# A Haar-domain channel mix as two half-height products, and column transforms as one full-precision product

## The chip, the core and the metric

The kernel runs on one core of one Trainium2 chip. The metric is the device time of one execution in microseconds (us). The engines are called PE (TensorE, the matrix engine; PEld is its weight load), DVE (VectorE), ACT (ScalarE), POOL (GpSimd) and SP (SyncE). SP and ACT issue the DMAs here.

## The reference

The input x has 4 images of 64 channels and 256 x 256 pixels. Four layers are applied in a row. Layers 0, 1 and 3 are long convolutions: for each channel a separable filter, a product of a row filter and a column filter that come out of a small sine network, is convolved with the image (causally: the FFT of twice the size makes it a plain convolution cut to 256 x 256), and the input times a bias per channel is added. Layer 2 works in the Haar domain:

```python
f1 = haar2d(x)
acc = 0
for i in range(2):
    f3 = f1 * v[i]
    f4 = einsum('bchw,oc->bohw', f3, conv_w[i])
    f5 = sign(f4) * relu(abs(f4) - tau[i])
    acc = acc + f5
y = haar2d(acc, inverse=True) + x
```

v and tau have one value per pixel of the coefficient image, and conv_w[i] is a 64 x 64 matrix over the channels. So at every coefficient the 64 channels are mixed by two matrices, thresholded, and the two results are added.

## The kernel before, in words

**Convolutions.** For one image b and one channel c, `contract` (L187) multiplies the 256 x 256 image with a Toeplitz matrix read from a padded filter in DRAM. It issues, for each of two halves of the output rows, one product with 256 columns (L190) and one with 128 (L191), both in full 32-bit precision, which PE executes as two instructions each. Layer 0 and layer 1 take two contractions each. `first` copies the result out of PSUM on ACT (L199), `second` adds bias times input on DVE (L212).

**Forward Haar transform.** `pairs` (L253) makes the first row level on DVE (L257, L258), `store` keeps a copy in DRAM, `levels` (L263) makes the other row levels on DVE. The column transform `down` (L283) is one product with a 128 x 128 matrix of signs. A channel in the set `in_parts` is first split: `split` (L276) rounds the 128 x 512 tile to fp32r on ACT (L280) and takes the rest on DVE (L281), and `down` then runs two fp32r products with `hbr` on the two exact parts (L288). A channel outside the set takes one full-precision product with `hbt` instead. Before the change every channel of every image is in `in_parts`. The result is copied by ACT (L296) and stored to DRAM (coef).

**Mixing.** `mixing` (L316) takes a group of four coefficient rows at a time, 64 groups per image. `load` brings a tile f with (row half k, channel c) on the 128 partitions, two such rows q, 256 columns. `mix` (L335) multiplies, for q and for each half h of the columns, the 128 x 128 block of f (as weights) with `wb`, a 128 x 256 block-diagonal matrix that holds the 64 x 128 pair of channel matrices twice and zeros elsewhere (L340). The result px fills two banks of PSUM. DVE (L357) and ACT (L359) multiply it with v, 64 elements at a time on ACT: 12 of 16 blocks for images 0 to 2, 6 for image 3. `shrink` takes the absolute value and the sign on ACT (L365, L366) and subtracts tau on DVE (L367), `signed` finishes the threshold on DVE (L372), `add` adds the two results into the SBUF array z on DVE (L376).

**Inverse.** `inverse` (L386) gathers one channel at a time out of z on ACT (zc, L396), transforms rows (L403, L404) and columns (L416), adds the kept input and runs layer 3 on two thirds of the channels; for images 0 to 2 the other third (`put_off`) is stored and its layer 3 is run during the mixing of image 3.

**Order.** All work is put on a list of events with a tick, a place within the tick, and a function; the list is sorted and issued, so that the order on each engine is fixed by ticks written out by hand. The mixing of image b has one group per tick. Beside it run the convolutions of image b + 1, spread over the ticks from shortly before the mixing to its end; channels of the last two blocks of four are stretched out into the inverse (`border`). In image 3 the layer 3 convolutions put off earlier run beside the mixing.

Of the kernel before, what the change touches and what calls it, by code (L numbers as in the profile page):

```python
# [9 lines left out]
F32 = mybir.dt.float32  # L10
# [6 lines left out]
B, C, S, EMB, ORD = 4, 64, 256, 33, 64  # L17
P = 128
# [19 lines left out]
def conv_seq_kernel(ctx, tc, x, fz, fw, bias, decay, haar, haar_row, factors, vt, taut, wmix, out):  # L38
# [14 lines left out]
    nc = tc.nc  # L53

    const = ctx.enter_context(tc.tile_pool(name="const", bufs=1))
# [3 lines left out]
    zpool = ctx.enter_context(tc.tile_pool(name="zpool", bufs=1))  # L59
# [4 lines left out]
    psx = ctx.enter_context(tc.tile_pool(name="psx", bufs=2, space=PSUM))  # L64
# [4 lines left out]
    hbr = const.tile([P, P], F32R, name="hbr")  # L69
    hrow = const.tile([P, 2, P], F32, name="hrow")  # L70
    hsinv, ident = hrow[:, 0, :], hrow[:, 1, :]
    wb = const.tile([P, 2, P], F32, name="wb")
    bsb = const.tile([P, 3, C], F32, name="bsb")


    z = zpool.tile([P, 2, S, C], F32, name="z")

    sd = zpool.tile([P, 8, 2, 2, P], F32, name="sd")
    keep = [dram.tile([C, P, 2, 2, P], F32, name=f"keep{b}") for b in range(B)]
# [4 lines left out]

    room = z.rearrange("p h r c -> p (h r c)")
    free = [0]

    def part(n, parts=P):  # L90
# [57 lines left out]
    def constants():  # L148
        signs = part(P)
        nc.sync.dma_start(hbt, haar[0])  # L150
        nc.sync.dma_start(signs, haar[1])
        nc.sync.dma_start(hrow, haar_row)
        nc.vector.memset(wb, 0.0)
        for r in range(2):
            nc.sync.dma_start(wb[r * C : (r + 1) * C, r, :], wmix)
        nc.scalar.copy(hb, signs)
        nc.scalar.copy(hbr, hbt)

# [57 lines left out]

    def butterfly(b):

        d = mx.tile([P, 2, C], F32, name=f"bfly_{b}", tag="mag")
        nc.vector.tensor_sub(d, z[:, :, 0, :], z[:, :, 1, :])  # L220
        nc.vector.tensor_add(z[:, :, 0, :], z[:, :, 0, :], z[:, :, 1, :])
        nc.vector.tensor_copy(z[:, :, 1, :], d)

# [90 lines left out]
    def mixing(b, start, n_act):  # L316

        st = {}

        def load(g):  # L320
            f = mx.tile([P, 2, S], F32, name=f"f_{b}_{g}", tag="f", bufs=3)
            nc.sync.dma_start(f, coef[b].rearrange("k c p w -> (k c) p w")[:, 2 * g : 2 * g + 2])
            st[g] = {"f": f}
            if g % GT == 0:
                t = mx.tile([P, 2, GT, 16], F32, name=f"vt_{b}_{g}", tag="vt")
                nc.sync.dma_start(t, scales[g // GT])
                st["vt", g // GT] = t

        def scale(g, i):
            return st["vt", g // GT][:, i, g % GT, :]  # L330

        def over(g, i, n):
            return scale(g, i)[:, :n].unsqueeze(2).to_broadcast([P, n, C])

        def mix(g):  # L335
            f = st[g]["f"]
            ps = psx.tile([P, 2, 2, S], F32, name=f"px_{b}_{g}", tag="mix")
            for q in range(2):
                for h in range(2):
                    nc.tensor.matmul(  # L340
                        ps[:, h, q, :],
                        f[:, q, h * P : (h + 1) * P],
                        wb.rearrange("p r n -> p (r n)"),
                        start=True,
                        stop=True,
                    )
            if g == 0:

                one, two = ps[:, :, 0, :P], ps[:, :, 0, P:]
                d = mx.tile([P, 2, P], F32, name=f"d_{b}", tag="mag")  # L350
                nc.vector.tensor_copy(d, two)
                nc.vector.tensor_sub(two, one, d)
                nc.vector.tensor_add(one, one, d)
            f4 = mx.tile([P, 16, C], F32, name=f"f4_{b}_{g}", tag="f4")
            px = ps.rearrange("p h q (r i o) -> p (h q r i) o", r=2, i=2)
            n = 16 - n_act
            nc.vector.tensor_tensor(f4[:, :n], px[:, :n], over(g, 0, n), ALU.mult)  # L357
            for j in range(n, 16):
                nc.scalar.mul(f4[:, j], px[:, j], scale(g, 0)[:, j : j + 1])  # L359
            st[g]["f4"] = f4  # L360

        def shrink(g):
            f4 = st[g]["f4"]
            mag = mx.tile([P, 16, C], F32, name=f"mag_{b}_{g}", tag="mag")
            nc.scalar.activation(mag, f4, AF.Abs)  # L365
            nc.scalar.activation(f4, f4, AF.Sign)  # L366
            nc.vector.tensor_sub(mag, mag, over(g, 1, 16))  # L367
            st[g]["mag"] = mag

        def signed(g):  # L370
            mag = st[g]["mag"]
            nc.vector.scalar_tensor_tensor(mag, mag, 0.0, st[g]["f4"], ALU.max, ALU.mult)  # L372

        def add(g):
            parts = st.pop(g)["mag"].rearrange("p (h r i) o -> p h r i o", h=2, i=2)
            nc.vector.tensor_add(z[:, :, 4 * g : 4 * g + 4, :], parts[:, :, :, 0, :], parts[:, :, :, 1, :])  # L376

        for g in range(S // 4):
            at(start + g - 2, 0, load, g)

            for s, (place, stage) in enumerate([(-2.5, mix), (-3.5, shrink), (-4.1, signed), (-4.2, add)]):
                at(start + g + s, place, stage, g)

    def inverse(b, start, put_off):  # L386

        st = {}

        def fetch(c):  # L390
            if c == 0:
                butterfly(b)
            r = mx.tile([P, 2, 2, P], F32, name=f"r_{b}_{c}", tag="f", bufs=3)
            nc.sync.dma_start(r, keep[b][c])
            a = mx.tile([P, 2, 2, P], F32, name=f"zc_{b}_{c}", tag="mag")
            nc.scalar.copy(a, z[:, :, :, c].rearrange("p h (i k) -> p h k i", k=2))  # L396
            st[c] = {"r": r, "z": a}

        def rows(c):
            a = st[c]["z"]  # L400
            ps = psm.tile([P, 2, 2, P], F32, name=f"pw_{b}_{c}", tag="mm")
            for m in range(2):
                nc.tensor.matmul(ps[:, m, 0, :], a[:, 0, m, :], hsinv, start=True, stop=True)  # L403
                nc.tensor.transpose(ps[:, m, 1, :], a[:, 1, m, :], ident)  # L404
            w = mx.tile([P, 2, 2, 2, P], F32R, name=f"w_{b}_{c}", tag="f4")
            nc.scalar.copy(w[:, 0], ps)  # L406
            nc.vector.tensor_tensor(w[:, 1], ps, w[:, 0].bitcast(F32), ALU.subtract)
            st[c]["w"] = w
            if c not in put_off:
                st[c][2] = toeplitz(2, c, f"t2_{b}_{c}")  # L410

        def cols(c):
            ps = psm.tile([P, 2, 2, P], F32, name=f"pu_{b}_{c}", tag="mm")
            flat = "p m e w -> p (m e w)"
            for i in range(2):
                nc.tensor.matmul(  # L416
                    ps.rearrange(flat), hb, st[c]["w"][:, i].rearrange(flat), start=(i == 0), stop=(i == 1)
                )
            t = io.tile([P, 2, 2, P], F32, name=f"t_{b}_{c}", tag="res", bufs=BUFS["res"])
            nc.vector.scalar_tensor_tensor(t, st[c]["r"], 0.5, ps, ALU.mult, ALU.add)  # L420
            u = io.tile([P, 2, S], F32, name=f"u_{b}_{c}", tag="y", bufs=BUFS["y"])
            v = u.rearrange("p m (w e) -> p m w e", e=2)
            nc.vector.tensor_add(v[:, :, :, 0], t[:, :, 0, :], t[:, :, 1, :])
            nc.vector.tensor_sub(v[:, :, :, 1], t[:, :, 0, :], t[:, :, 1, :])
            st[c]["u"] = u

        ends = last(b, st)
        for c in range(C):

            at(start + c, -1, fetch, c)  # L430
            at(start + c + 1, -9, rows, c)
            at(start + c + 2, -8, cols, c)
            if c in put_off:
                at(start + c + 3, -5, lambda c: nc.scalar.dma_start(late[b, c], st.pop(c)["u"]), c)
            else:
                for s, stage in enumerate(ends):
                    at(start + c + 3 + s, s - 7, stage, c)
# [22 lines left out]
    def spread(begin, end, n=C):  # L460
        return [begin + i * (end - begin - 1) // (n - 1) for i in range(n)]
# [4 lines left out]
    one, two, three = filters(0, nc.scalar), filters(1, nc.scalar), filters(2, nc.sync)  # L466
# [20 lines left out]
    for b in range(B):  # L487
        mixing(b, start, 12 if b + 1 < B else 6)
        end = start + groups + 3
        if b + 1 < B:  # L490
            ready = convolutions(b + 1, spread(ahead, end + 2), in_parts=range(C), border=end)
        else:
            convolution(
                [(i, c) for i in range(B - 1) for c in sorted(put_off)], spread(start - 2, end + 2, (B - 1) * len(put_off))
            )
        inverse(b, end, put_off if b + 1 < B else ())

        start = max(end + C, ready + 3)
        ahead = start - 3
# [111 lines left out]
```

## Time and profile before

| | us |
|---|---|
| median of 3 runs | 2974.68 (2972.39 to 2974.85) |
| profiled execution, its own time | 2975.2 |
| profiled execution, span | 2973.4 |
| PE busy | 2913.8 (98%) |
| PE weight loads busy | 2615.1 (88%) |
| DVE busy | 2545.5 (86%) |
| ACT busy | 2156.9 (73%) |

The span runs from the first to the last instruction of the profiled execution; its own time also holds what lies around the span. TensorE's granted clock is full throughout. The mixing of image 0 lies from about 453 to 860 us, of image 1 from 1092 to 1526, of image 2 from 1766 to 2206, of image 3 from 2436 to 2708; the inverse stages lie between and after them.

In a line of a group the columns are: source line, engine, operation, output and inputs by name, weights' and moving shapes, count, then busy us, mean ns of one, and after the second bar the idle time of the engine just before, with what ended it. In a timeline line they are start, length, engine, line, operation, names, shapes and how many were merged.

### The profile page before, as it was taken

Reading aid. Unit: us, or ns where it says so; the run is one execution under the profiler, and the core shown is the slowest. Engines: PE = TensorE matmul, PEld = TensorE weight load, DVE = VectorE, ACT = ScalarE, POOL = GpSimd, SP = SyncE. Lnnn points to the kernel's source line nnn. Section 1 sums busy time; section 2 is a strip of 40 time slices with the busy share of each in tenths; the row PEclk is TensorE's granted clock in tenths of the full one; section 3 lists DMA queues with packets and bytes.
Section 4 is the critical chain, followed back from the end, with each engine's and each line's share of the span. In section 5 each row is a group of like instructions: output and inputs, shape, how many; then the busy total and the mean of one; then the engine's idle time right before and its main releaser. Section 6 shows DMA issues by size and latency. Waiting matters only on the chain. (4 is left out here: it accounts for less than half of the span.)

```text
span 2973.4 us, 52066 instructions
## 1 busy us (share of the span) xinstructions
PE 2913.8 (98%) x16950; PEld 2615.1 (88%) x16950; DVE 2545.5 (86%) x4571; ACT 2156.9 (73%) x5014; POOL 0.2 (0%) x4
## 2 busy tenths in 40 slices
PE   8999999999999999999999999999999999999999
PEld 6898988888888898888888988888888988888998
DVE  5766768999998879999989879999998889998776
ACT  2333338999986758889986668989986768887554
POOL 0000000000000000000000000000000000000000
PEclk9999999999999999999999999999999999999999
DMA  5877777666667876776777876777777878777676
GB/s 159 247 237 226 229 228 212 203 202 207 207 196 244 250 217 200 208 216 204 208 219 244 250 225 197 209 210 211 207 216 237 256 236 235 233 230 217 212 212 186
DMA packets 562497, 649.73 MB, mean 219 GB/s; under 512 B 44369, under 2 KB 447412, under 8 KB 562100
## 3 DMA queue, kind: packets, MB, share of 16 engines
q1 hardware_dynamic: 482996, 562.07, 64.8%
q10 hardware_dynamic: 79232, 84.34, 8.0%
q8 instruction: 137, 2.24, 0.3%
q14 instruction: 132, 1.08, 0.1%
HBM read 426.77 MB, written 219.48 MB: 217 GB/s over the span
## 5 line engine op out<-in xcount | busy, mean ns | idle before, releaser
L190 PE MATMUL py<-t,a 128*128 128x256 f32 x3072 | 919.0, 381 | 8.9 <-ACT a L199 5.5
L199 ACT COPY a<-pa 128x512 f32<-128x512 f32 x768 | 477.2, 621 | 387.9 <-PE pa L191 357.2
L359 ACT ACTIVATE f<-px,vt 128x64 f32<-128x64 f32 x2688 | 582.3, 358 | 143.5 <-DVE f L357 143.4
L191 PEld LDWEIGHTS py<-t,a 128*128 128x128 f32 x3072 | 583.4, 190 | 79.3
L191 PE MATMUL py<-t,a 128*128 128x128 f32 x3072 | 590.0, 274 | 0.0
L190 PEld LDWEIGHTS py<-t,a 128*128 128x128 f32 x3072 | 500.4, 191 | 50.9 <-ACT a L199 12.4
L340 PE MATMUL px<-wb,f 128*128 128x256 f32 x2048 | 488.2, 380 | 4.9 <-ACT f L359 4.9
L340 PEld LDWEIGHTS px<-wb,f 128*128 128x128 f32 x2048 | 369.5, 190 | 47.0 <-ACT f L359 6.7
L367 DVE TENSOR_TENSOR mag<-mag,vt 128x1024 f32<-128x1024 f32 x256 | 312.4, 1220 | 28.3 <-ACT mag L365 26.9
L190 PE MATMUL pa<-t,y 128*128 128x256 f32 x1024 | 311.6, 386 | 22.4 <-DVE y L212 20.3
L406 ACT CAST w<-pw 128x512 fp32r<-128x512 f32 x256 | 150.2, 587 | 227.0 <-PE pw L404 218.9
L372 DVE SCALAR_TENSOR_TENSOR mag<-mag,f 128x1024 f32<-128x1024 f32 x256 | 311.7, 1218 | 1.9
L190 PE MATMUL pa<-t,x 128*128 128x256 f32 x1024 | 305.9, 380 | 0.4 <-issue 0.4
L365 ACT ACTIVATE mag<-f 128x1024 f32<-128x1024 f32 x256 | 293.7, 1147 | 11.0 <-DVE z L376 8.8
L366 ACT ACTIVATE f<-f 128x1024 f32<-128x1024 f32 x256 | 285.2, 1114 | 3.0
L396 ACT COPY zc<-z 128x512 f32<-128x512 f32 x256 | 282.0, 1103 | 0.7 <-ACT w L406 0.4
L281 DVE TENSOR_TENSOR sp<-sd,sp 128x512 fp32r<-128x512 f32 x256 | 176.1, 688 | 91.4 <-ACT sp L280 90.2
L190 PE MATMUL pa<-t,u 128*128 128x256 f32 x772 | 232.8, 383 | 2.9 <-PE pu L416 1.6
L420 DVE SCALAR_TENSOR_TENSOR t<-r,pu 128x512 f32<-128x512 f32 x256 | 174.9, 683 | 60.4 <-PE pu L416 57.0
L212 DVE SCALAR_TENSOR_TENSOR y<-x,bsb,py 128x512 f32<-128x512 f32 x256 | 190.1, 742 | 37.9 <-PE py L191 36.1
L212 DVE SCALAR_TENSOR_TENSOR y<-y,bsb,py 128x512 f32<-128x512 f32 x256 | 190.0, 742 | 34.2 <-PE py L191 33.1
L191 PEld LDWEIGHTS pa<-t,x 128*128 128x128 f32 x1024 | 194.6, 190 | 26.3
(67 smaller groups left out, 4458.9 us busy)
## 6 DMA issues: line engine op xcount, KB each, us to landing
t<-pad SPq DMA_DIRECT2D x768, 256.0 KB, 3.9
x<-in_x SPq DMA_DIRECT2D x256, 256.0 KB, 3.6
keep<-sd SPq DMA_DIRECT2D x256, 256.0 KB, 2.9
coef<-co SPq DMA_DIRECT2D x256, 256.0 KB, 3.3
f<-coef SPq DMA_DIRECT2D x256, 256.0 KB, 3.2
r<-keep SPq DMA_DIRECT2D x256, 256.0 KB, 3.3
out_y<-y ACTq DMA_DIRECT2D x256, 256.0 KB, 3.6
late<-u ACTq DMA_DIRECT2D x63, 256.0 KB, 2.9
```

The source lines that it names most:

```text
L190: nc.tensor.matmul(ps[:, m, :], src[:, 0, m * P : (m + 1) * P], t[:, ::-1], start=True, stop=False)
L191: nc.tensor.matmul(ps[:, m, P:], src[:, 1, m * P : (m + 1) * P], t[:, : P - 1 : -1], start=False, stop=True)
L199: nc.scalar.copy(a, ps)
L212: nc.vector.scalar_tensor_tensor(y, s[res], bsb[:, layer, c : c + 1], ps, ALU.mult, ALU.add)
L281: nc.vector.tensor_tensor(w[:, 1], t, w[:, 0].bitcast(F32), ALU.subtract)
L340: nc.tensor.matmul(ps[:, h, q, :], f[:, q, h * P : (h + 1) * P], wb.rearrange("p r n -> p (r n)"), start=True, stop=True,)
L359: nc.scalar.mul(f4[:, j], px[:, j], scale(g, 0)[:, j : j + 1])
L365: nc.scalar.activation(mag, f4, AF.Abs)
L366: nc.scalar.activation(f4, f4, AF.Sign)
L367: nc.vector.tensor_sub(mag, mag, over(g, 1, 16))
L372: nc.vector.scalar_tensor_tensor(mag, mag, 0.0, st[g]["f4"], ALU.max, ALU.mult)
L396: nc.scalar.copy(a, z[:, :, :, c].rearrange("p h (i k) -> p h k i", k=2))
```

## The change

The channel mix no longer multiplies 128 rows with a block-diagonal matrix. `wb` holds the 64 x 128 pair of channel matrices twice, once on partitions 0 to 63 and once on 64 to 127, with no zeros. Each block of f is multiplied in two products of 64 rows and 128 columns, one for each half r of the partitions. The result has r as its outermost index, so that the two halves lie in different banks of PSUM. z, the scales and the factors follow with a new order of indices (r, h, q, i); sizes stay.

The set `in_parts` gets smaller beside the mixing. For image 0 it still holds all channels. For image 1 it holds channels 56 to 63. For images 2 and 3 it holds channels 56 to 63 and the even channels below 56. The other channels take the existing path with one full-precision product, and their `split` isn't issued.

```diff
-    wb = const.tile([P, 2, P], F32, name="wb")
+    wb = const.tile([P, P], F32, name="wb")
-    z = zpool.tile([P, 2, S, C], F32, name="z")
+    z = zpool.tile([P, 2, 2, P, C], F32, name="z")
...
-        nc.vector.memset(wb, 0.0)
         for r in range(2):
-            nc.sync.dma_start(wb[r * C : (r + 1) * C, r, :], wmix)
+            nc.sync.dma_start(wb[r * C : (r + 1) * C], wmix)
...
         def mix(g):
             f = st[g]["f"]
-            ps = psx.tile([P, 2, 2, S], F32, name=f"px_{b}_{g}", tag="mix")
-            for q in range(2):
-                for h in range(2):
-                    nc.tensor.matmul(
-                        ps[:, h, q, :],
-                        f[:, q, h * P : (h + 1) * P],
-                        wb.rearrange("p r n -> p (r n)"),
-                        start=True,
-                        stop=True,
-                    )
+            ps = psx.tile([P, 2, 2, 2, P], F32, name=f"px_{b}_{g}", tag="mix")
+            for h in range(2):
+                for q in range(2):
+                    for r in range(2):
+                        rows = slice(r * C, (r + 1) * C)
+                        nc.tensor.matmul(
+                            ps[:, r, h, q, :], f[rows, q, h * P : (h + 1) * P], wb[rows], start=True, stop=True
+                        )
...
-            px = ps.rearrange("p h q (r i o) -> p (h q r i) o", r=2, i=2)
+            px = ps.rearrange("p r h q (i o) -> p (r h q i) o", i=2)
...
         def add(g):
-            parts = st.pop(g)["mag"].rearrange("p (h r i) o -> p h r i o", h=2, i=2)
-            nc.vector.tensor_add(z[:, :, 4 * g : 4 * g + 4, :], parts[:, :, :, 0, :], parts[:, :, :, 1, :])
+            parts = st.pop(g)["mag"].rearrange("p (s q i) o -> p s q i o", q=2, i=2)
+            rows = z.rearrange("p r h i c -> p (r h) i c")[:, :, 2 * g : 2 * g + 2, :]
+            nc.vector.tensor_add(rows, parts[:, :, :, 0, :], parts[:, :, :, 1, :])
...
-            nc.scalar.copy(a, z[:, :, :, c].rearrange("p h (i k) -> p h k i", k=2))
+            nc.scalar.copy(a, z[:, :, :, :, c].rearrange("p k h i -> p h k i"))
...
-            ready = convolutions(b + 1, spread(ahead, end + 2), in_parts=range(C), border=end)
+            in_parts = [c for c in range(C) if c >= C - 8 or (b > 0 and c % 2 == 0)]
+            ready = convolutions(b + 1, spread(ahead, end + 2), in_parts=in_parts, border=end)
```

The butterfly over the first two rows of z and of px is written with the new indices, and the host lays out v, tau and the factors to match.

More of the change, by code (lines that the diff above doesn't have):

```diff
@@ L83, in conv_seq_kernel @@
     late = dram.tile([B, C, P, 2, S], F32, name="late")
-    room = z.rearrange("p h r c -> p (h r c)")
+    room = z.rearrange("p r h i c -> p (r h i c)")
     free = [0]
@@ L217, in butterfly @@
     def butterfly(b):
+        one, two = z[:, 0, :, 0, :], z[:, 1, :, 0, :]
         d = mx.tile([P, 2, C], F32, name=f"bfly_{b}", tag="mag")
-        nc.vector.tensor_sub(d, z[:, :, 0, :], z[:, :, 1, :])
-        nc.vector.tensor_add(z[:, :, 0, :], z[:, :, 0, :], z[:, :, 1, :])
-        nc.vector.tensor_copy(z[:, :, 1, :], d)
+        nc.vector.tensor_sub(d, one, two)
+        nc.vector.tensor_add(one, one, two)
+        nc.vector.tensor_copy(two, d)
     events = []
@@ L336, in mix @@
             f = st[g]["f"]
-            ps = psx.tile([P, 2, 2, S], F32, name=f"px_{b}_{g}", tag="mix")
-            for q in range(2):
-                for h in range(2):
-                    nc.tensor.matmul(
-                        ps[:, h, q, :],
-                        f[:, q, h * P : (h + 1) * P],
-                        wb.rearrange("p r n -> p (r n)"),
-                        start=True,
-                        stop=True,
-                    )
+            ps = psx.tile([P, 2, 2, 2, P], F32, name=f"px_{b}_{g}", tag="mix")
[6 more added lines that the diff above has]
+                        )
             if g == 0:
-                one, two = ps[:, :, 0, :P], ps[:, :, 0, P:]
+                one, two = ps[:, 0, :, 0, :], ps[:, 1, :, 0, :]
                 d = mx.tile([P, 2, P], F32, name=f"d_{b}", tag="mag")
@@ L570, in coefficients @@
         a = a.reshape(2, S, S)[:, down][:, :, along]
-        return lay(a.reshape(2, S // 4, 4, 2, P).transpose(4, 1, 3, 2, 0).reshape(P, S // 4, 16))
+        return lay(a.reshape(2, S // 4, 2, 2, 2, P).transpose(5, 1, 3, 4, 2, 0).reshape(P, S // 4, 16))
     local = _haar_local()
@@ L576 @@
     scaled = (half * np.float32(math.sqrt(0.5)))[level]
-    rows = np.repeat(np.abs(local).max(axis=1), 2).reshape(1, S // 4, 1, 4, 1)
+    rows = np.abs(local).max(axis=1).reshape(1, S // 4, 1, 1, 2, 1)
     signs = np.sign(local)
@@ L580 @@
         [
-            (rows**power * np.stack([first, np.full(P, second)], axis=1).reshape(P, 1, 2, 1, 1) * np.ones((1, 2))).reshape(
+            (rows**power * np.stack([first, np.full(P, second)], axis=1).reshape(P, 1, 1, 2, 1, 1) * np.ones((2, 1, 1, 2))).reshape(
                 P, S // 4, 16
```

## The prediction

> **What bounds the kernel now.** I first read the page's engine shares: PE is busy 98% of the span, DVE 86%, ACT 73%. An average cannot price this change, which touches the four mixing stages only, so I next took busy times by stretch. A stretch runs from the first channel-mix product (L340) of a batch to the last.
>
> ```profile
> 453.50:860.30 406.80, 397.36 (x2181) 351.50 (x2180) 388.11 (x672) 375.88 (x1079) 0.00 (x0) 1.00 0.68 205
> ...
> 1092.00:1526.40 434.40, 428.79 (x2398) 384.84 (x2397) 402.89 (x709) 380.82 (x1075) 0.00 (x0) 1.00 0.71 207
> ...
> 1766.00:2206.50 440.50, 434.95 (x2430) 390.14 (x2430) 408.25 (x717) 387.31 (x1093) 0.00 (x0) 1.00 0.71 208
> ...
> 2436.00:2708.00 272.00, 266.85 (x1439) 237.28 (x1438) 265.30 (x310) 234.15 (x554) 0.00 (x0) 1.00 0.79 234
> ```
>
> After the length come busy us of PE, PE's weight loads, DVE and ACT, then POOL, the clock, DMA share and GB/s. PE is idle for 9.4, 5.6, 5.6 and 5.2 us. Batches 0 to 2 are bound by PE, with DVE's busy share only 2 to 6 points behind; batch 3 is held by DVE as much as by PE (265.3 and 266.9 of 272). In batch 0, 8.1 of PE's 9.4 idle us wait for DVE's y (L212), by the waits of that stretch.
>
> Then the groups that the change touches: mix products, their weight loads, and the subtraction of the split.
>
> ```profile
> L340 PE MATMUL px<-wb,f 128*128 128x256 f32 x2048 | 488.2, 380 | 4.9 <-ACT f L359 4.9
> ...
> L340 PEld LDWEIGHTS px<-wb,f 128*128 128x128 f32 x2048 | 369.5, 190 | 47.0 <-ACT f L359 6.7
> ...
> L281 DVE TENSOR_TENSOR sp<-sd,sp 128x512 fp32r<-128x512 f32 x256 | 176.1, 688 | 91.4 <-ACT sp L280 90.2
> ```
>
> A full-precision product is two instructions. Mean durations overlap and overstate a product, so I price PE by starts in the timeline (start, length, engine, line).
>
> ```profile
> 453.52 1.89 PE L340 MATMUL px<-wb,f 128*128 128x256 f32 x8
> 455.25 0.59 PE L190 MATMUL py<-t,a 128*128 128x256 f32 x2
> 455.68 0.39 PE L191 MATMUL py<-t,a 128*128 128x128 f32 x2
> ...
> 457.64 0.39 PE L191 MATMUL pa<-t,x 128*128 128x128 f32 x2
> 457.78 0.71 PE L288 MATMUL pz<-sp,hbr 128*128 128x512 f32 x2
> 458.33 0.59 PE L190 MATMUL py<-t,a 128*128 128x256 f32 x2
> ```
>
> One group's mix takes 455.25 - 453.52 = **1.73 us**, eight instructions of 0.216. A pair of 256 columns takes 0.43 (455.25 to 455.68), and a pair of 128 columns 0.22 as pairs follow each other, so 0.11 an instruction. The fp32r pair of a column transform takes 458.33 - (457.64 + 0.22) = **0.47 us**.
>
> The decisive view is one accident of the start-up: the third filter's first product contracts over 33 rows, and stands between full-height products. Below it is a control at the same place, the same filter's next product with 128 rows.
>
> ```profile
> 64.14 0.38 PE L191 MATMUL pa<-t,x 128*128 128x128 f32 x2
> 64.46 0.70 PE L112 MATMUL fp<-z 33*128 33x256 f32 x2
> 65.08 0.70 PE L190 MATMUL py<-t,a 128*128 128x256 f32 x2
> 65.62 0.38 PE L191 MATMUL py<-t,a 128*128 128x128 f32 x2
> ...
> 75.45 0.38 PE L191 MATMUL pa<-t,x 128*128 128x128 f32 x2
> 75.67 0.60 PE L114 MATMUL fp<-z 128*128 128x256 f32 x2
> 76.10 0.59 PE L190 MATMUL py<-t,a 128*128 128x256 f32 x2
> 76.53 0.38 PE L191 MATMUL py<-t,a 128*128 128x128 f32 x2
> ```
>
> From L191 to L191 the control needs 1.08 us, the 33-row visit 1.48. The **0.40 us** is two changes of the array's height, 0.20 each. The weight loads show how:
>
> ```profile
> 64.46 0.29 PEld L112 LDWEIGHTS fp<-z 33*128 33x128 f32 x2
> 65.08 0.30 PEld L190 LDWEIGHTS py<-t,a 128*128 128x128 f32 x2 [0.33 <-issue]
> ```
>
> Elsewhere a load starts about 0.11 us ahead of its product; here it starts with it, so it wasn't pulled forward: about 0.1 us of draining and 0.1 us of a bare load, on the way in and on the way out. No data wait stands there.
>
> **What the Trainium skill says.** "TensorEngine Tiling (Array Packing)", Key Properties: a change of tiling mode drains TensorE, and tiles can load weights and multiply in parallel. The 0.40 us agrees with the first; no run here shows the second. Gotcha 1 of that page: row tiles running together must write different PSUM banks; the new layout of px puts the halves r in separate 2 KB banks. "TensorE: Matmul & The Clock Gate", LDWEIGHTS: a load takes as long as its columns, whatever its rows. The trace agrees: 183 to 190 ns for 33 and for 128 rows. Part 3 of that page: products of different row groups overlap while starting in program order; its packed examples count products, and don't say whether the loads go at once.
>
> **The change part by part.**
>
> *Mix.* Four products of 128 rows and 256 columns become eight of 64 rows and 128 columns, in the order half 0, half 1. That is 16 instructions and 16 loads for 8 and 8, over the same columns. One after another they would take 16 x 0.108 = 1.73 us, so all gain is overlap. In order, the two instructions of half 0 follow each other (they share rows), and the first of half 1 starts beside the second of half 0. If loads of different halves overlap too, one product of each half costs 0.22 us. Four such are 0.88, the last half sticks out by 0.11, and the changes of height cost 0.40: **1.40 us** for 1.73, a gain of **0.33** a group. The wait added is this drain: behind it in PE's queue stands the next contraction, whose copy (ACT L199) or y (DVE L212) comes later by the same 0.2. Bounds for the unseen overlap: none, 1.73 + 0.40 = 2.13; loads alone in series, 16 x 0.107 + 0.40 = 2.11; drains hidden, 0.99. I take 1.40: the skill states the overlap and the trace the drain.
>
> *Column transforms.* Those not in parts lose the cast (ACT L280) and the subtraction (DVE L281, 0.60 us between starts in the timeline). They get one full-precision product of 512 columns, a path the trace doesn't show: twice the 256-column pair, 0.86 us for 0.47, so **+0.39** each on PE. The bounds are close: no less than this streaming, and no more than 0.1 over it, for a bare load. For batch 1, c below 56 are converted (56), for batches 2 and 3 odd c below 56 (28 each): 112 in all. L281 ran 49, 49 and 50 times in the first three stretches, so some 49, 24 and 24 lie there and 15 outside.
>
> *The rest.* The new index order of z, scales and px keeps element counts. The gather zc (ACT L396) reads z at half the stride. Its 1.10 us against 0.62 for a plain copy bounds it at -0.5 to +0.5 us; the inverse stage, where ACT is busy about 65% and PE fully, covers it. If that cover went, 256 x 0.5 = 128 us would be the ceiling. The addition into z (L376, 0.69 us) could move by 0.1 us either way, up to 6 us in batch 3, where DVE has no cover. One memset goes, at start-up. No DMA is added or moved on any queue.
>
> *Sum on PE.* Batch 0: 64 x 0.33 = -21, 49 x 0.39 = +19, and some 5 of the 8 us of waits for y, as DVE sheds 49 x 0.6 = 29: -7. Batches 1 and 2: -21 + 24 x 0.39 = -12, and 2 of their 5 us of waits: -14 each. Batch 3: PE sheds 21, but DVE sheds nothing and has 6.7 us free: -3. Outside: 15 x 0.39 = +6. Together **-32 us**. The profiled execution took 2975.2 us (span 2973.4), 0.5 over the median, so 2943 for either. A measurement can tell about 0.2%, 6 us, from no change.
>
> **The rivals.**
>
> *Loads in series* (slower). If weight loads of the two halves share one path, 16 loads at 0.107 set the pace: 2.11 us, +0.38 on each of 256 groups is +97, the transforms add 112 x 0.39 = +44, and DVE's relief returns 10: 3106. For it: loads depend on columns alone, and 128-column products already run at the loads' pace. Against: a 64-row load uses only its own rows. It decides from where a group's gain falls under 0.17 us (192 x 0.17 pays for 44 - 12), that is, a mix over 1.56 us or a step over 0.26 instead of 0.22. This is also the case of a change that doesn't do what it says.
>
> *Part overlap.* A step of 0.25 to 0.32 a pair, a mix of 1.5 to 1.8 us: 2963 to 3025.
>
> *Drains hidden, DVE the next bound.* A mix of 0.99 gains 0.74; batch 0 then gains 28, and DVE (402.9 - 24 x 0.6 = 388, at its present saturation some 400) stops batches 1 and 2 at -33. With -3 and +6: 2884. Against it stands the 33-row visit.
>
> **How the numbers follow.** Forecast 2943, own range 2918 to 2963: 0.65. Loads in series: 0.17. Part overlap: 0.11, split over same and slower. Drains hidden: 0.07. Faster: 0.65 less 0.01, plus 0.07 and 0.01, 0.72; slower: 0.17 plus 0.05, 0.22; same: 0.06. The range 2895 to 3005 leaves out the loads in series and little else.
>
> **What would show it.** Right: px products of 64 rows x4096, the two halves' starts a few ns apart in the timeline, 1.3 to 1.5 us from the first to the next contraction, loads after each change not ahead of their product; L281 down to 144; a transform near 0.86; DVE near 98% in batch 3, unchanged in length. Wrong: px starts evenly 0.11 apart over 1.7 us, or a contraction right behind a mix with its load pulled ahead.

## The result, and the profile after

The changed kernel takes **3042.86 us** (median, 3037.95 to 3043.86) against 2974.76: a ratio of 1.0225, interval 1.0207 to 1.0243, 68 us slower where 32 us faster were forecast, and outside the range. Its profiled execution took 3043.86 us, with a span of 3042.0.

In the busy times by stretch (columns as before: length, PE, PE's loads, DVE, ACT, POOL, clock, DMA share, GB/s) the stretches are again from the first mix of a batch to the last.

```profile
454.00:884.30 430.30, 394.91 (x2693) 326.57 (x2692) 365.42 (x629) 357.12 (x1030) 0.00 (x0) 0.99 0.64 192
1118.50:1577.90 459.40, 427.14 (x2943) 364.87 (x2942) 397.61 (x693) 373.16 (x1068) 0.00 (x0) 0.99 0.66 199
1813.80:2271.10 457.30, 426.65 (x2942) 365.12 (x2942) 397.50 (x693) 372.93 (x1068) 0.00 (x0) 0.99 0.66 200
2503.00:2776.40 273.40, 244.31 (x1948) 212.29 (x1948) 265.92 (x310) 234.10 (x554) 0.00 (x0) 0.98 0.80 232
```

Before, they were 406.8, 440.9, 440.5 and 271.8 us long. The second one of the prediction ended one group early; in full it is:

```profile
1092.00:1532.90 440.90, 435.17 (x2432) 390.26 (x2431) 408.61 (x717) 387.29 (x1093) 0.00 (x0) 1.00 0.71 207
```

In each of the first three, PE, DVE and ACT are all *less* busy than before, and yet the stretch is 17 to 24 us longer: 23.5 + 18.5 + 16.8 + 1.6 = 60 us of the 68. PE's idle time rose from 9 to 35 us in the first. This is a loss by waiting, not by work.

The two operations themselves did what was forecast, or better. First one mix in the timeline, products and loads:

```profile
605.06 0.38 PE L190 MATMUL pa<-t,y 128*128 128x128 f32 x2
...
605.37 0.97 PEld L343 LDWEIGHTS px<-wb,f 64*128 64x128 f32 x16
605.38 1.16 PE L343 MATMUL px<-wb,f 64*128 64x128 f32 x16
...
606.47 0.70 PE L189 MATMUL py<-t,a 128*128 128x256 f32 x2
```

The 16 loads take 0.97 us from the first start to the last end. One after another, at the 0.107 of the prediction, they would take 1.71: the halves load at once. From the end of the contraction (605.06 + 0.22) to the next one's effective start (606.47 + 0.10 for its bare load) there are **1.29 us** for the mix, with both changes of height, against 1.73; that is also the median of all mixes. The forecast was 1.40. Then one full-precision transform:

```profile
608.97 0.39 PE L190 MATMUL pa<-t,x 128*128 128x128 f32 x2
609.19 1.02 PE L292 MATMUL pz<-sd,hbt 128*128 128x512 f32 x2
610.05 0.59 PE L189 MATMUL py<-t,a 128*128 128x256 f32 x2
```

It takes 610.05 - 609.19 = **0.86 us**, as forecast. So PE was relieved of more than was worked out. What went up is in the waits of the whole kernel (total us, times, longest us), PE's own first, then DVE's, then ACT's:

```profile
PE pa L189 <- DVE y L211: 61.0, 77, 2.0
PE py L189 <- ACT a L198: 49.4, 61, 1.9
```

```profile
DVE mag L366 <- ACT mag L364: 143.0, 104, 2.8
```

```profile
ACT f L358 <- DVE f L356: 251.3, 183, 3.7
```

The same four before:

```profile
PE pa L190 <- DVE y L212: 20.3, 33, 1.7
PE py L190 <- ACT a L199: 5.5, 8, 1.5
DVE mag L367 <- ACT mag L365: 26.9, 37, 2.8
ACT f L359 <- DVE f L357: 143.4, 157, 3.6
```

PE waits for y and a, and DVE and ACT wait for each other. The timeline shows a late y being made. Its contraction ended at 600.2 us (two L190 from 599.84); DVE then does this:

```profile
600.07 0.64 DVE L270 SCALAR_TENSOR_TENSOR sd<-sd 128x256 f32<-128x256 f32 x1
600.62 0.42 DVE L257 TENSOR_TENSOR sd<-y 128x256 f32<-128x256 f32 x1
600.95 0.42 DVE L258 TENSOR_TENSOR sd<-y 128x256 f32<-128x256 f32 x1
601.29 0.39 DVE L269 TENSOR_TENSOR sd<-sd 128x128 f32<-128x128 f32 x1
601.59 0.42 DVE L356 TENSOR_TENSOR f<-px,vt 128x256 f32<-128x256 f32 x1
601.92 1.22 DVE L366 TENSOR_TENSOR mag<-mag,vt 128x1024 f32<-128x1024 f32 x1
603.06 0.74 DVE L211 SCALAR_TENSOR_TENSOR y<-x,bsb,py 128x512 f32<-128x512 f32 x1
```

```profile
603.90 0.67 PE L189 MATMUL pa<-t,y 128*128 128x256 f32 x2 [1.50 <-issue]
```

DVE is never idle here, but y, whose input is ready since 600.2, starts only at 603.06 and ends at 603.80. PE stands still for 1.5 us; its next product, which reads y, starts at 603.90. (The profile puts this wait down to "issue"; that it is y is read from the times.) Comparing the instruction lists of the two programs shows what changed. The builder that turns the list of events into queues does not keep the list's order: it plans each engine's order anew. PE follows the list but for a few places; on DVE, of the 4458 instructions that both programs share, 1624 stand in another place than before, on ACT 1279 of 5225. Around group 24 of the first mixing DVE's lists read (tiles with their group or channel; y0 and y1 add bias times input, sd is one row level step, sp a split; f, mag, signed and z are a group's multiplication, subtraction of tau, last threshold step and addition):

```
before: f24 signed23 z y1:27 pairs pairs f25 sp21 mag24 y0:28 signed24 sd z sd sp22 f26 mag25
        y0:29 signed25 sd z y1:28 sd pairs sp23 pairs mag26 f27
after:  f24 signed23 z y1:27 pairs pairs mag24 f25 signed24 y0:28 sd z sd sd sd mag25 f26
        signed25 y0:29 sd z sd sd sd sd sd sd sd mag26 y1:28 signed26 pairs pairs f27
```

Two things changed: level steps stand in front of y (of those listed, twelve precede y1:28 where three did), and f of the next group has slipped behind mag.

### The profile page after: what moved, and what is told of

It is laid out like the page before. It is cut to its first block, busy times and chain, and to the rows that moved or that the text cites. A ratio compares the mean times of both kernels' runs of the same rounds, so it can differ in the third digit from the quotient of the medians.

```text
span 3042.0 us, 55766 instructions
## 1 busy us (share of the span) xinstructions
PE 2879.0 (95%) x18998; PEld 2516.0 (83%) x18998; DVE 2492.6 (82%) x4458; ACT 2103.4 (69%) x4902; POOL 0.2 (0%) x4
## 5 line engine op out<-in xcount | busy, mean ns | idle before, releaser
L189 PE MATMUL py<-t,a 128*128 128x256 f32 x3072 | 946.3, 390 | 55.5 <-ACT a L198 49.4
L190 PEld LDWEIGHTS py<-t,a 128*128 128x128 f32 x3072 | 586.2, 191 | 80.3
L189 PEld LDWEIGHTS py<-t,a 128*128 128x128 f32 x3072 | 484.4, 191 | 152.6 <-ACT a L198 72.6
L190 PE MATMUL py<-t,a 128*128 128x128 f32 x3072 | 592.6, 275 | 0.0
L366 DVE TENSOR_TENSOR mag<-mag,vt 128x1024 f32<-128x1024 f32 x256 | 312.8, 1222 | 144.3 <-ACT mag L364 143.0
L189 PE MATMUL pa<-t,y 128*128 128x256 f32 x1024 | 318.0, 392 | 68.9 <-DVE y L211 61.0
L343 PE MATMUL px<-wb,f 64*128 64x128 f32 x4096 | 305.3, 287 | 14.4 <-ACT f L358 12.1
L189 PE MATMUL pa<-t,x 128*128 128x256 f32 x1024 | 310.8, 385 | 2.2 <-DMA t<-pad 1.3
L343 PEld LDWEIGHTS px<-wb,f 64*128 64x128 f32 x4096 | 254.3, 189 | 47.9 <-ACT f L358 16.7
L189 PEld LDWEIGHTS pa<-t,y 128*128 128x128 f32 x1024 | 157.1, 192 | 96.4 <-DVE y L211 81.5
L189 PE MATMUL pa<-t,u 128*128 128x256 f32 x772 | 232.8, 383 | 3.9 <-PE pu L416 1.4
L190 PEld LDWEIGHTS pa<-t,y 128*128 128x128 f32 x1024 | 196.3, 192 | 27.0
```

The lines of the kernel that those rows point to most:

```text
L189: nc.tensor.matmul(ps[:, m, :], src[:, 0, m * P : (m + 1) * P], t[:, ::-1], start=True, stop=False)
L190: nc.tensor.matmul(ps[:, m, P:], src[:, 1, m * P : (m + 1) * P], t[:, : P - 1 : -1], start=False, stop=True)
L343: nc.tensor.matmul(ps[:, r, h, q, :], f[rows, q, h * P : (h + 1) * P], wb[rows], start=True, stop=True)
```

## The experiments

Two theories. **Order**: the time is lost by the new places on DVE and ACT. **Path**: it is lost by the longer transform on PE, in whatever order. The means to tell them apart is an edge between two instructions of one engine that fixes which is issued first and adds no wait. To hold an engine to the order of before, each of its instructions gets an edge to the one that preceded it there:

```diff
+def pin(nc, tc):
+    for engine, text in ORDER.items():
+        mine = [i for i in traced if str(i.engine).split(".")[-1] == engine]
...
+            if before is not None:
+                why = mybir.DependencyInfo(mybir.DependencyClass.NoSync, mybir.DependencyReason.DATA)
+                tc.add_manual_dep(mine[at], before.name, why, reason="pin")
+            before = mine[at]
...
         conv_seq_kernel(tc, *args)
+        pin(nc, tc)
```

### The change in the order of before (e1_order)

The edit is `pin` with ORDER holding DVE, ACT and SP.

> The changed kernel, every operation as changed, with DVE, ACT and SP held to the order that the kernel before gave them (the 112 splits left out of it). In the changed kernel the builder put 1624 of 4458 DVE instructions and 1279 of 5225 on ACT into other places. Order theory (the new places cost the time; the mix itself gains): a mix stays at 1.29 us against 1.73, so by PE's sum some 2920 to 2950 us, PE's waits for y and a back near 20 and 6 us. Path theory (the full-precision transform, 0.39 us longer, lies on the chain that ends last, in whatever order): 3030 to 3045.

Measured: **2945.36 us**, ratio to before 0.9899 (0.9884 to 0.9914). The same operations are 97 us faster in the old order. The path theory falls. The waits of this run, PE's and then DVE's (`pin` moves line numbers up by 21, so L210 is L189 of the changed kernel):

```profile
PE pa L210 <- DVE y L232: 31.7, 41, 2.1
PE py L210 <- ACT a L219: 22.4, 35, 2.0
```

```profile
DVE mag L387 <- ACT mag L385: 37.8, 50, 2.8
```

The first is about half of what it is in the changed kernel, the other two are less than half. PE's two are above the 20 and 6 us that were expected, the second nearly four times as long. PE is now faster in the mixes and may catch up with y and a more often; no run tests this.

### Each part alone, in the builder's order (e2_half, e3_full)

```diff
e2_half:
-            in_parts = [c for c in range(C) if c >= C - 8 or (b > 0 and c % 2 == 0)]
+            in_parts = range(C)
e3_full, in the kernel before:
-            ready = convolutions(b + 1, spread(ahead, end + 2), in_parts=range(C), border=end)
+            in_parts = [c for c in range(C) if c >= C - 8 or (b > 0 and c % 2 == 0)]
+            ready = convolutions(b + 1, spread(ahead, end + 2), in_parts=in_parts, border=end)
```

> The half-height mix alone: all channels stay split, in_parts=range(C). Here too the builder chooses the order (865 DVE places differ from before). Path theory: without the longer transform this gains; PE loses 0.44 us a group, so 2900 to 2950. Order theory: what the builder's order costs here isn't known beforehand; with fewer places moved, between 2920 and 3010.

> The full-precision transforms alone, with the mix of before: PE gets 112 x 0.39 = 44 us more. If PE's sum decides in the order of before, 3010 to 3020. Path theory: most of the change's loss and no gain, so 3050 or more. Order theory: 44 us and the builder's new order (1475 DVE places moved): 3030 to 3080.

Measured: e2_half 2990.12 us, ratio 1.0049 (1.0034 to 1.0064); e3_full 3034.08, ratio 1.0199 (1.0184 to 1.0214). The half-height mix alone, with PE relieved in 256 groups, gains nothing and is 15 us slower than before. The transforms alone bring most of the loss, and they move more of DVE's places (1475 against 865). Both times lie in the ranges of the order theory and outside those of the path theory. But the order theory's ranges were wide, and PE's work changes along with the order here, so both were run in the old order too.

### Each part alone, in the order of before (e4_half_order, e7_full_order)

> The half-height mix alone, with DVE, ACT and SP held to the order of before. Both theories: a gain. By PE's sum 192 groups x 0.44 = 84 us at most, but DVE is busy 93 to 95% of the stretches already: 2900 to 2950. If it is no faster than before, neither theory holds, and the drain or DVE's own chain eats the gain.

> The full-precision transforms alone, mix as before, with DVE, ACT and SP held to the order of before. PE's sum: 112 x 0.39 = 44 us more, less some of PE's 16 us of waits in the first three mixing stretches, as DVE and ACT are relieved: 3003 to 3019. If it stays at the 3034 of the builder's order, that order costs nothing without the half-height mix.

Measured: e4_half_order 2980.99 us, ratio 1.0017 (1.0010 to 1.0024), against an expected gain of 25 to 75 us: a miss, and by its own last sentence one under which neither theory holds. e7_full_order 2991.80, ratio 1.0062 (1.0047 to 1.0077), some 17 us slower than before and 42 less than in the builder's order, also under the 29 to 44 us expected. The first stretch of e4_half_order, then of e7_full_order, then of e1_order:

```profile
453.30:861.40 408.10, 376.78 (x2692) 326.50 (x2692) 387.09 (x671) 375.76 (x1077) 0.00 (x0) 1.00 0.68 203
```

```profile
453.60:864.70 411.10, 410.27 (x2181) 352.67 (x2181) 363.60 (x623) 356.91 (x1030) 0.00 (x0) 1.00 0.66 201
```

```profile
452.90:846.00 393.10, 384.60 (x2693) 322.54 (x2692) 360.00 (x623) 354.04 (x1030) 0.00 (x0) 1.00 0.71 211
```

With the mix alone PE is busy for 21 us less than before, so the drain didn't eat the gain; PE is idle for 31 us instead of 9, of which 19.3 wait for DVE's y and 10.8 for ACT's a. DVE stands at the 387 us it had before (388.1), 95% of the stretch, ACT at 376, and the stretch is as long as before. So DVE, with ACT, now holds the stretch; which of the two would have to be relieved isn't tested. The order theory thus accounts for the 97 us between the changed kernel and e1_order, not for this. With the transforms alone DVE sheds 24 us, but now PE is busy for 410 of 411. Only both together shorten the stretch, by 13.7 us: in the order of before the parts cost 6 and 17 us alone and gain 30 together.

### Which engine's order (e5_dve_order, e6_act_order)

The edit is `pin` on the changed kernel, with ORDER holding one engine.

> The changed kernel with DVE alone held to the order of before; the builder chooses ACT's and SP's (737 of 5225 ACT places still differ from before). Order theory, with DVE's order as the cause: within 10 us of the 2945 with all three held. If ACT's order is the cause: near 3040.

> The changed kernel with ACT alone held to the order of before; the builder chooses DVE's (1431 of 4458 DVE places still differ). With DVE's order as the cause: 3020 to 3045. With ACT's: near 2945.

Measured: 2956.37 us, ratio 0.9941 (0.9925 to 0.9958), with DVE held; 3038.49, ratio 1.0219 (1.0204 to 1.0234), with ACT held. DVE's order is worth 3042.9 - 2956.4 = 87 of the 97 us, ACT's alone 4, which is within the spread of the changed kernel's own runs. The run with DVE held lies 11 us above e1_order, just outside the 10 that were expected. It isn't quite DVE alone: with DVE held, some of ACT's places return too (737 differ instead of 1279).

### Which places on DVE (e8_levels, e9_f, e10_f_levels)

The edit adds edges for some instructions only; `BEHIND` lists them.

```diff
+def hold(nc, tc):
...
+        tc.add_manual_dep(mine[at], mine[at - steps[k + 1]].name, why, reason="hold")
```

> The changed kernel in the builder's order, with one thing held: the row level steps of the Haar transform (sd, L269 and L270), which it moved ahead of y, pairs and mag on DVE. Each run of them now stays behind the DVE instruction that it followed before the change (509 edges of order, no wait). If those steps are the cause: 2945 to 2975. If it is the order of the rest: over 3010.

> The changed kernel in the builder's order, with one thing held on DVE: the first multiplication of the next group, f (L356), stays ahead of the last threshold step of this group, mag (L371), in 133 groups and ahead of mag's subtraction (L366) in 91, wherever the kernel before had it so; in the changed kernel it fell behind L371 in more than half of the groups of batches 1 and 2 (27 of 63 are still ahead, 51 before). If that turn costs most of the 97 us: 2960 to 2990. If only the level steps with it do: over 3010.

> Both holds at once on DVE: the level steps (509 edges) and f (224 edges); 581 of 4458 DVE places still differ from before. If these two turns are the cause on DVE: 2950 to 2970, near the 2956 with DVE held whole. If it stays over 3000, the cause is in the rest, or in no single turn.

Measured: level steps held 3022.62 us, ratio 1.0165 (1.0149 to 1.0180); f held 3012.73, ratio 1.0122 (1.0105 to 1.0139); both held **2966.67**, ratio 0.9958 (0.9945 to 0.9971). Both single holds missed the range in which their turn would be the cause, and lie over 3010: neither turn alone is most of the loss. Held alone they give back 20 and 30 us, together 76 of 97, more than their sum. Why isn't shown. One reason can be read from the built programs: with the level steps held alone, f stands ahead of the last threshold step in even fewer groups (21 of 63 in batch 1, against 27 in the changed kernel). The mere number of moved places doesn't decide: counted like the 1624 above, 998 DVE places differ with the level steps held, 1564 with f held.

Nor does PE's wait for y follow the times. With the level steps held it rose from 61.0 us to 83.8, though the run is 20 us faster:

```profile
PE pa L203 <- DVE y L225: 83.8, 82, 2.0
DVE mag L380 <- ACT mag L378: 115.9, 120, 2.8
```

And e4_half_order has 74.0 us of it at 2981. DVE's wait of mag for ACT follows them better: 143.0 us in the changed kernel, 115.9 with the level steps held, 109.7 with f held, 65.2 with both, 37.8 in e1_order, 26.9 before. So the late y of the timeline above is one form of the loss and not its measure.

So the loss is settled as DVE's order, and most of it as two turns in it: row level steps in front of y, and the next group's f behind this group's threshold. By which wait each turn costs its time is not settled, and why the builder chose these places isn't shown by any run here.

## Why the prediction was wrong

**The step that failed** is the term of waits in the sum on PE: "some 5 of the 8 us of waits for y" given back in batch 0, "2 of their 5" in batches 1 and 2. It let the 112 splits only disappear and kept every other instruction of DVE in its place, since the text before it takes for granted that "the order on each engine is fixed by ticks written out by hand". It isn't: 1624 of DVE's 4458 instructions changed places, and their order is worth 87 of the 97 us between the changed kernel and e1_order. In batch 0 the terms for PE's work came out: -21 + 19 = -2, and PE's busy time fell from 397.4 to 394.9. But PE's idle time, instead of falling by 5 from 9, rose to 35, of which 20.7 us are waits for y (8.1 before, 5.8 in e1_order), and the stretch grew by 23.5 us instead of shrinking by 7. Either part of the change alone made the builder plan another order (e2_half, e3_full); that the order of before suits this machine better than the new one is measured, but not explained. In the order that was assumed, the forecast of 2943 us meets the 2945.36 of e1_order.

**That agreement is partly luck.** The other three stretches of e1_order, behind the first one shown above:

```profile
1076.50:1508.50 432.00, 417.72 (x2942) 360.48 (x2942) 393.77 (x692) 375.00 (x1068) 0.00 (x0) 1.00 0.72 212
1743.40:2174.30 430.90, 417.32 (x2942) 360.41 (x2942) 394.03 (x693) 375.01 (x1068) 0.00 (x0) 1.00 0.72 212
2406.10:2677.60 271.50, 241.99 (x1949) 210.40 (x1948) 264.60 (x310) 233.35 (x554) 0.00 (x0) 0.98 0.80 234
```

The forecast for the four was -7, -14, -14 and -3 us; the run shows -13.7, -8.9, -9.6 and -0.3. The total fits because two errors offset each other. The term "64 x 0.33" was too small as an operation: the mix took 1.29 us, not 1.40, as both halves start at once and the last half doesn't stick out by 0.11; 192 groups x 0.44 would be 84 us. But PE's time wasn't freed one for one. DVE was taken as no limit until some 400 us of a stretch, while in e4_half_order, with DVE at 95% and ACT at 92% of batch 0, 21 us less work on PE shortened nothing. In the order of before the parts' times don't add up. In the builder's they nearly do (15 and 59 us against 68), but each of those runs has an order of its own.

**Right, step by step.** The transform (0.86 us). The price of two changes of height, read from one 33-row product in the start-up: it lies in the 1.29. L281 at 144 instead of 256. Batch 3 unchanged within 2 us (3 less were forecast), as DVE's busy time there stayed at 265 to 266 us while PE shed 22. The gather and the addition into z kept their 1.10 and 0.68 us, so the new strides cost nothing.

**The rivals.** Loads in series is refuted: 16 loads in 0.97 us. "TensorEngine Tiling (Array Packing)", Key Properties, said that tiles can load and multiply in parallel, and this trace now agrees, with those 0.97 us. Part overlap is refuted too: the mix took 1.29 us, under its 1.5 to 1.8. The slower result came by a way that no rival named, and the range ended 38 us short of it.

## What to carry to other kernels

Where the tool that builds the program chooses the order on the engines, a change that adds, removes or reshapes instructions can be two changes, and the second one can be larger than the first; compare the instruction lists of before and after ahead of any sum of durations. Here, with PE, DVE and ACT busy for 98, 95 and 92% of the first stretch, relieving PE alone bought nothing, and the order on DVE decided more than the operations did. A loss with less work on every engine calls for one run in the old order: here it turned a change that was 2.2% slower into a version 1.0% faster than the kernel before, the fastest of all that were run.

## What the runs showed of the hardware that was not expected

The two row halves start together, loads and products alike: in the trace of the mix above each product of the second half starts 7 ns after its partner of the first, and 16 loads of 64 rows fit into 0.97 us. (The 8 loads of 128 rows before took 1.60, but each of them stood behind a product of 256 columns.)

TensorE's clock was granted at 1.000 over the execution before but 0.994 in the changed kernel, 0.98 in its fourth stretch, though the waits of PE there are short: the longest is 2.6 us (px for ACT's f). The trace of the changed kernel has the clock at half speed in 11 pieces of 3.41 us. In the 3.41 us ahead of each of them PE was busy for only 23 to 51% of the time, with one idle gap of 1.7 to 2.6 us; ahead of the last, it was busy for 0.78 of the 3.40 us up to 2765.4, and the clock was 0.50 in the next 3.40. "TensorE: Matmul & The Clock Gate", Why this matters for your kernels, warns of idle gaps over some 3 us; here shorter ones were enough, at 89% busy over the stretch. The clock isn't the main cause of the loss: 11 x 3.41 us at half speed are at most 19 us, e6_act_order is nearly as slow at 0.996, and e3_full takes 3034 us at a full 1.000.
